# Two edits to the order of a two-layer graph network: where the differences of the gate weights are queued, and how many gate graphs the third group runs among the next layers

## The chip, the cores and the metric

The kernel runs on one core of a Trainium2 chip. The metric is device microseconds of one execution; the figure given for a kernel is the median of its runs. The engines are called as the profile calls them: PE (matrix products, with PEld for its weight loads), DVE (vector), ACT (scalar), POOL and SP, whose queue issues most of the transfers.

## The reference, cut to what matters

64 graphs of 256 nodes with 256 features pass two layers, each with a residual and a layer norm.

```
# layer 0
h = (norm_adj + max(alpha, 1e-10) * I) @ x;  x = layernorm(x + h @ W.T + b)
# layer 1
h  = relu(bn1(conv1(x)))                       # 1x1
xc = relu(bn2(conv2(h)) + x)                   # 17 taps along the nodes
s  = x @ w_se.T + b_se;  A = exp(-|s_i - s_j|^2) * adj
xm = A @ relu(x @ w_msg.T + b_msg)
gi = concat(xc, xm) @ w_ih.T + b_ih;  gh = x @ w_hh.T + b_hh
r = sigmoid(gi_r + gh_r);  z = sigmoid(gi_z + gh_z);  n = tanh(gi_n + r * gh_n)
x  = layernorm(x + (1 - z) * n + z * x)
```

All is float32.

## The kernel before, in words

The 64 graphs are worked in `NQ = 4` groups of `Q = 16`. For a group there are three kinds of work.

- **Layers**: `layer0(g)` and `layer1(g)` for each graph. `layer1` ends with the message part `xn` written to DRAM, and leaves the forward transform of `h` in `V`. Its products are in order `p_x1T`, `p_conv`, `p_msg`, `p_dft`, `p_rows`, `p_dist`, `p_nmp`; those of `layer0` are `p_adjT`, `p_hT`, `p_out` (L398, read by DVE at L403).
- **Transform**: the 17-tap convolution is a product in frequency space, `products(step)` for 12 steps (`p_real`, `p_k`, with the transformed taps `u` streamed from DRAM), and then an inverse transform on DVE, `real_transform`, `complex_begin` and `complex_end`. The last has 58 pieces, called `end`, and writes `xc_d`.
- **Gates**: `gru(g)` for each graph, in four pieces (`yield` ends one): `p_rz` products, more of them with the transposes `p_xcT` of the next graph, and two halves `p_n`. The first graph of a group has four pieces more, which load its inputs. For `p_rz` a product of two by two blocks is done with seven block products in place of eight; that needs sums of the inputs (`sums`, on POOL) and differences of the weights (`T1` to `T4` of `wrz`, four DVE instructions at L948), made once.

The pieces of different kinds are interleaved by hand, with generators. In `graphs(first, part, V, others)`, which runs the layers of the graphs in `part`, a piece of `others[i]` is called after the first and the sixth piece of `layer1`, and pieces of `layer0` of the graph two further on after the second, fifth and sixth. `take(stage, n)` gives n pieces of a stage. In the first group, `others` holds the 13 parts of the transformed taps (`weights`), for graphs 0 to 12, and one piece of `gate_weights` for each of the graphs 13, 14 and 15: the loads of the weights, an empty piece, and the differences.

The text order gives each instruction its rank. A planner then fixes the order on each engine before the run: where an engine has nothing of higher rank ready by the planner's own costs, an instruction of lower rank that is ready goes first. [...] `with tc.issue_after(i):` ties each instruction of its block behind `i` on `i`'s engine. `mark(op)` puts certain DVE instructions on the list `marks`: in `layer0` the two at L403, in `layer1` those of `h`, `msg` and `aT`, and in `gru` five, among them `first` (L809). `paced(main, end, rate)` empties the list after each piece of `main` and ties `rate` pieces of `end` behind each mark on it; outside `paced` the list only grows.

After the transform of group q come the layers of group q+1 from graph `AHEAD` on, with the first gates of group q (`early`) in `others`: five pieces a call for q = 0, two for q = 1 and 2. What `early` leaves follows at once. The other gates of group q (`late`) run in the transform of group q+1: some pieces between the steps of its products (for the last group one at each odd step, six in all), the rest as `main` of `paced`. For the last group `main` is `late` alone, at 1.35 pieces for each mark:

```
elif more:
    run(paced(chain(merge(take(late, 20), take(begin, 6), 3), begin), end, RATES[q]))
else:
    run(paced(late, end, RATES[q]))
    run(end)
```

`AHEAD` is 12 for the second group and 6 for the third and fourth; the gates of the last group run at the end, alone.

Of the kernel before, what the change touches and what calls it, by code (L numbers as in the profile page):

```python
# [20 lines left out]
def bcast_rows(v, n, rows=P):  # L21

    return bass.AP(tensor=v.tensor, offset=v.offset, ap=[[0, rows], [1, n]])
# [3 lines left out]
def kernel(  # L27
# [27 lines left out]
    nc = tc.nc  # L55
# [10 lines left out]
    Q = P // GT  # L66
# [20 lines left out]
    marks = []  # L87
# [7 lines left out]
    def load(g):  # L95
        if g >= B:
            return
        ain[g] = loads.tile([P, NCH, N], F32, name="adj_t")
        nc.sync.dma_start(ain[g], adj[g].rearrange("(c p) m -> p c m", p=P))
        xin[g] = loads.tile([P, NCH, D], F32, name="x_t")  # L100
        nc.sync.dma_start(xin[g], x[g].rearrange("(c p) f -> p c f", p=P))
# [40 lines left out]
    wrz = const.tile([P, 7, HALF, D], F32)  # L142
    B11, B21, B22, T1, T2, T3, T4 = range(7)
# [116 lines left out]
    def load_taps(pool, n):  # L260

        if n == NPARTS:
            return
        ng = GW // NPARTS
        tp = TAPS_OF[n] = pool.tile([KT, ng, D], F32, name="taps", bufs=2)

        def taps(c, t, count, step):

            channel = min(c * GW + n * ng, D - ng)
            return bass.AP(  # L270
                tensor=conv2T.tensor, offset=conv2T.offset + (channel * TAPS + t) * D,
                ap=[[step * D, count], [TAPS * D, ng], [1, D]],
            )

        for c in range(GC):
            nc.sync.dma_start(tp[c * TR : (c + 1) * TR], taps(c, 0, TR, 1))
        nc.sync.dma_start(tp[GC * TR : KT - 1], taps(0, TR, GC - 1, GW * TAPS))
        nc.sync.dma_start(tp[KT - 1 :], taps(GC - 1, TR, 1, 1))
# [461 lines left out]
    def load_conv(g):  # L740
        CONV[g] = gate.tile([P, NCH, D], F32, name="xc_g")
        nc.sync.dma_start(CONV[g], xc_d[g // Q][g % Q].rearrange("(c p) d -> p c d", p=P))
# [8 lines left out]
    def residual(g):  # L751

        nc.gpsimd.dma_start(  # L753
            CONV[g], x1_d[g // Q][g % Q].rearrange("(c p) d -> p c d", p=P), accum_op=ALU.add
        )
# [108 lines left out]
    def merge(main, other, every=1):  # L864

        for i, _ in enumerate(main):
            yield
            if i % every == every - 1 and next(other, "end") != "end":
                yield
        yield from other  # L870
# [5 lines left out]
    def take(stage, n):  # L876

        for _ in range(n):
            if next(stage, "end") == "end":
                return  # L880
            yield
# [6 lines left out]
    def run(stage):  # L888
        for _ in stage:
            pass  # L890
# [18 lines left out]
    def graphs(first, part, V, others):  # L909


        for i in part:
            load(first + i + 3)
            given = {"layer0": layer0(first + i + 2) if first + i + 2 < B else iter(()), "other": others[i]}
            for piece, _ in enumerate(layer1(first + i, V, i)):
                yield
                for name in PLACES[piece]:
                    if next(given[name], "end") != "end":
                        yield
            yield from given["other"]  # L920

    with tc.tile_pool(name="setup", bufs=1) as setup:
        load_taps(setup, 0)
        nc.sync.dma_start(wmsg, w_msgT.rearrange("(k p) o -> p k o", p=P))
        nc.sync.dma_start(bmsg_t, bcast_rows(b_msg, D))
        firsts = merge(layer0(0), layer0(1))
        run(take(firsts, 2))
        load(2)
        tables(setup)
        run(firsts)  # L930
        scale2 = next(batch_norms(setup))

        def gate_weights():
            for b, half_inputs, cols in ((B11, 0, 0), (T1, 0, 1), (B21, 1, 0), (B22, 1, 1)):
                at = slice(cols * D, (cols + 1) * D)
                if half_inputs == 0:
                    parts = ((slice(0, DCH), w_hhT), (slice(DCH, HALF), w_ihT[D : D + P]))
                else:
                    parts = ((slice(0, 1), w_ihT[D + P :]), (slice(1, HALF), w_ihT[:D]))
                for k, w in parts:  # L940
                    nc.sync.dma_start(wrz[:, b, k], w[:, at].rearrange("(k p) o -> p k o", p=P))
            for k, w in ((0, w_hhT), (DCH, w_ihT[D:]), (2 * DCH, w_ihT[:D])):
                nc.sync.dma_start(wn[:, k : k + DCH], w[:, 2 * D :].rearrange("(k p) o -> p k o", p=P))
            yield
            yield

            for to, a, b in ((T3, B22, T1), (T1, T1, B11), (T2, B22, T1), (T4, B21, T2)):
                nc.vector.tensor_sub(wrz[:, to], wrz[:, a], wrz[:, b])  # L948
            yield

        more_weights = gate_weights()
        others = [weights(setup, i, scale2) for i in range(NPARTS)]
        others += [take(more_weights, 1) for i in range(NPARTS, Q)]
        run(graphs(0, range(Q), V, others))
        bih_t = setup.tile([P, 3 * D], F32, name="bih", tag="taps", bufs=2)
        nc.sync.dma_start(bih_t, bcast_rows(b_ih, 3 * D))
        bhh_t = setup.tile([P, 3 * D], F32, name="bhh", tag="taps", bufs=2)
        nc.sync.dma_start(bhh_t, bcast_rows(b_hh, 3 * D))
        brz = brz_t.rearrange("p i d -> p (i d)")
        nc.vector.tensor_add(brz, bih_t[:, : 2 * D], bhh_t[:, : 2 * D])  # L960
        nc.vector.tensor_sub(brz_t[:, 1], brz_t[:, 1], brz_t[:, 0])
        nc.vector.tensor_copy(bn_t[:, 0, :], bih_t[:, 2 * D :])
        nc.vector.tensor_copy(bn_t[:, 1, :], bhh_t[:, 2 * D :])
    ustream = ctx.enter_context(tc.tile_pool(name="ustream", bufs=6))
    EARLY = 4

    def open_ahead(graphs):

# [4 lines left out]
    def gates(q, part):  # L973

        for i in part:
            if i == 0:
                load_conv(q * Q)
                load_gate(q * Q)
                yield
                load_conv(q * Q + 1)  # L980
                residual(q * Q)
                yield
                transposed(q * Q)
                yield
                input_sums(q * Q)
                yield
            yield from gru(q * Q + i)

    def nothing():
        return iter(())  # L990
# [5 lines left out]
    late = nothing()  # L996
    for q in range(NQ):
        first = (q + 1) * Q
        more = q + 1 < NQ
        end = complex_end(q)  # L1000
        if more:
            if q:
                others = [take(late, 3 if i % 3 == 0 else 2) for i in range(AHEAD)]
            else:
                others = [nothing() for _ in range(AHEAD)]
            begin = graphs(first, range(AHEAD), V2, others)
        sums(0)
        real = real_transform()
        for step in range(STEPS):
            if step < 4:  # L1010
                run(products(step))
            else:
                run(merge(products(step), take(real, 1)))
                run(complex_begin(step))
            if q:
                run(take(late, (0, 1, 1, 1, 1, 1, 2, 1, 2, 1, 2, 1)[step] if more else step % 2))
            else:
                run(take(begin, 3))
        run(real)
        if not q:  # L1020
            run(paced(begin, end, RATES[q]))
# [5 lines that stand above are left out]
        if more:  # L1027
            run(late)
            run(end)
            for f in range(0, FL, 12):  # L1030
                nc.scalar.copy(V[:, f : f + 12, :, : AHEAD * GT], V2[:, f : f + 12])
            if q == 0:
                scope.close()
                gate = ctx.enter_context(tc.tile_pool(name="gate", bufs=2))
            early = gates(q, range(EARLY))
            others = [take(early, 5 if q == 0 else 2) for _ in range(Q)]
            run(graphs(first, range(AHEAD, Q), V, others))
            run(early)
            if q == 0:
                scope, AHEAD, V2 = open_ahead(6)  # L1040
                ctx.enter_context(scope)
            late = gates(q, range(EARLY, Q))
        else:
            run(gates(q, range(Q)))

# [52 lines left out]
```

## Time and profile before

| | |
|---|---|
| median of 3 runs | 2172.98 us (2172.46 to 2173.61) |
| profiled execution | 2174.33 us |
| its span, first to last instruction | 2172.5 us |
| mean granted PE clock | 0.989 |
| PE, DVE, ACT, POOL busy | 2064.0, 1550.7, 834.3, 664.2 us |
| HBM traffic | 200.62 MB read, 103.06 MB written |

A row of groups gives line, engine, operation, output and inputs, then count, busy time and mean duration. A row of waits names who waited for whom, with total, number and longest. A row of the timeline has start, duration, engine and line, and in brackets the idle time before it and what ended it. Rows of windows give a stretch's length and each engine's busy time in it. Matmul ends are modelled, so distances between starts say more than durations.

### The profile page before, as it was taken

What the parts mean: (1) busy time and instruction counts of PE and PEld (TensorE: products, weight loads), DVE (VectorE), ACT (ScalarE), POOL (GpSimd) and SP (SyncE); (2) the same over time, 40 slices, a digit from 0 to 9 for tenths busy, and PEclk for the clock granted to TensorE, in tenths of its full rate; (3) what the DMA queues carried; (4) which work ended last, traced back from release to release, by engine and by line L of the source; (5) the groups of instructions that cost most, each with busy time, mean ns of one, the idle gap of its engine ahead of it and who ended that gap; (6) DMA issues with size and microseconds to landing.
All of it is one profiled execution on the core that took longest, in us unless ns stands there. A gap on an engine that the chain in (4) does not pass through costs nothing. (4 is left out here: it accounts for less than half of the span.)

```text
span 2172.5 us, 29034 instructions
## 1 busy us (share of the span) xinstructions
PE 2064.0 (95%) x9805; PEld 1748.4 (80%) x9805; DVE 1550.7 (71%) x3691; ACT 834.3 (38%) x1847; POOL 664.2 (31%) x640
## 2 busy tenths in 40 slices
PE   7999999887999999999999999899999998999998
PEld 5788788776788887788888888778888887788887
DVE  5555568785568798775556989775555889977776
ACT  4566643455331122455453122346543112222222
POOL 2444310211431233313222133323231123444442
PEclk9999999999999999999999999999999999999999
DMA  4765656434337644344335754334334844444442
GB/s 129 223 194 178 216 185 207 154 125 141 97 112 226 194 123 122 107 119 121 104 99 175 208 163 116 110 117 132 101 97 124 250 117 122 120 123 107 112 101 60
DMA packets 251182, 305.65 MB, mean 141 GB/s; under 512 B 18174, under 2 KB 229714, under 8 KB 251034
## 3 DMA queue, kind: packets, MB, share of 16 engines
q1 hardware_dynamic: 183530, 200.46, 30.4%
q10 hardware_dynamic: 44480, 67.39, 8.7%
q0 software_dynamic: 23024, 35.95, 8.6%
q8 instruction: 78, 1.28, 0.2%
q14 instruction: 70, 0.57, 0.1%
HBM read 200.62 MB, written 103.06 MB: 140 GB/s over the span
## 5 line engine op out<-in xcount | busy, mean ns | idle before, releaser
L833 PE MATMUL p_n<-wn,inputs 128*128 128x256 f32 x1536 | 355.9, 385 | 11.0 <-DVE first L809 10.6
L796 PE MATMUL p_rz<-wrz,sums 128*128 128x256 f32 x1536 | 350.9, 382 | 3.2 <-POOL sums L775 2.3
L833 PEld LDWEIGHTS p_n<-wn,inputs 128*128 128x128 f32 x1536 | 289.1, 192 | 58.1 <-DVE first L809 14.5
L796 PEld LDWEIGHTS p_rz<-wrz,sums 128*128 128x128 f32 x1536 | 290.7, 191 | 48.2 <-issue 5.9
L796 PE MATMUL p_rz<-wrz,inputs 128*128 128x256 f32 x1152 | 271.7, 379 | 0.4 <-ACT inputs L766 0.4
L314 POOL TENSOR_TENSOR ln_rs<-ln_rs,neg_half 128x2 f32<-128x2 f32 x129 | 101.2, 784 | 527.9 <-DVE ln_rs L313 417.4
L796 PEld LDWEIGHTS p_rz<-wrz,inputs 128*128 128x128 f32 x1152 | 217.5, 190 | 30.3 <-ACT inputs L766 1.0
L845 ACT ACTIVATE nn<-gn 128x256 f32<-128x256 f32 x128 | 53.2, 416 | 333.2 <-DVE gn L842 333.0
L518 PE MATMUL p_k<-u,VM 128*128 128x256 f32 x736 | 175.3, 380 | 4.1 <-DMA u<-ud 3.3
L775 POOL TENSOR_TENSOR sums<-inputs 128x384 f32<-128x384 f32 x64 | 67.8, 1059 | 335.1 <-ACT inputs L766 327.0
L358 POOL TENSOR_TENSOR dis<-deg,neg_half 128x2 f32<-128x2 f32 x64 | 46.5, 726 | 402.6 <-DVE deg L356 395.6
L324 ACT ACTIVATE x_g<-x_g,ln_mr,ln_rs 128x256 f32<-128x256 f32 x128 | 70.0, 593 | 245.6 <-DVE ln_mr L322 242.0
L518 PEld LDWEIGHTS p_k<-u,VM 128*128 128x128 f32 x736 | 138.1, 190 | 25.7 <-DMA u<-ud 3.4
L428 PE MATMUL p_conv<-wc,xn 128*128 128x259 f32 x512 | 128.8, 394 | 19.6 <-ACT xn L420 18.5
L388 PE MATMUL p_hT<-adjT,x 128*128 128x256 f32 x512 | 126.6, 390 | 9.5 <-DVE msg L452 4.9
L381 POOL TENSOR_TENSOR x_t<-x_t,b_t 128x512 f32<-128x512 f32 x64 | 86.4, 1350 | 146.7 <-ACT x L380 89.3
L463 PE MATMUL p_dft<-fwd,h 128*128 128x240 f32 x512 | 117.8, 373 | 13.9 <-ACT h L432 13.0
L428 PEld LDWEIGHTS p_conv<-wc,xn 128*128 128x128 f32 x512 | 97.1, 194 | 39.8 <-ACT xn L420 24.1
L489 DVE TENSOR_TENSOR aT<-aT,adjT 128x512 f32<-128x512 f32 x64 | 44.3, 692 | 115.3 <-ACT aT L488 115.3
L398 PE MATMUL p_out<-w,hT 128*128 128x256 f32 x512 | 123.9, 385 | 2.5 <-ACT hT L393 2.1
L449 PE MATMUL p_msg<-wmsg,xn 128*128 128x256 f32 x512 | 121.3, 379 | 0.0
L494 PE MATMUL p_nmp<-aT,msg 128*128 128x256 f32 x512 | 121.1, 379 | 0.2 <-DVE aT L489 0.2
(154 smaller groups left out, 3894.9 us busy)
## 6 DMA issues: line engine op xcount, KB each, us to landing
u<-ud SPq DMA_DIRECT2D x284, 256.0 KB
xn_d<-xn ACTq DMA_DIRECT2D x64, 512.0 KB
inputs<-xn_d SPq DMA_DIRECT2D x64, 512.0 KB
ud<-u_set POOLq DMA_DIRECT2D x39, 480.0 KB, 6.2
adj_t<-in_adj_dram SPq DMA_DIRECT2D x64, 256.0 KB
x_t<-in_x_dram SPq DMA_DIRECT2D x64, 256.0 KB
x_d<-x ACTq DMA_DIRECT2D x64, 256.0 KB
xc_d<-VM SPq DMA_DIRECT2D x64, 256.0 KB
```

The source lines that it names most:

```text
L314: nc.gpsimd.tensor_tensor(rs[:, : len(chunks)], rs[:, : len(chunks)], neg_half[:, : len(chunks)], op=ALU.pow)
L324: nc.scalar.activation(y[:, c, :], y[:, c, :], AF.Identity, bias=mr[:, c : c + 1], scale=rs[:, c : c + 1])
L381: nc.gpsimd.tensor_tensor(x_t, x_t, b0_t.unsqueeze(1).to_broadcast([P, NCH, D]), op=ALU.add)
L388: nc.tensor.matmul(p[:, k, :], x1[:, mc, k * P : (k + 1) * P], adjT[:, mc, 1 - mc : 3 - mc, :].rearrange("p n q -> p (n q)"), start=mc == ...
L398: nc.tensor.matmul(p[:, c, :], hT[:, k, c * P : (c + 1) * P], w0[:, k, :], start=k == 0, stop=k == DCH - 1)
L428: nc.tensor.matmul(p, x1T[:, k, c * P : (c + 1) * P], wc1[:, k, :], start=k == 0, stop=k == DCH - 1)
L449: nc.tensor.matmul(p[:, c, :], x1T[:, k, c * P : (c + 1) * P], wmsg[:, k, :], start=k == 0, stop=k == DCH - 1)
L463: nc.tensor.matmul(p[:, t0 * FL : t1 * FL], h[:, c, k * P : (k + 1) * P], fwd[:, first : first + t1 - t0, :].rearrange("p t f -> p (t f)") ...
L494: nc.tensor.matmul(p[:, k, :], msg[:, mc, k * P : (k + 1) * P], aT[:, mc].rearrange("p n q -> p (n q)"), start=mc == 0, stop=mc == NCH - 1,)
L518: nc.tensor.matmul(p[:, j * D : (j + 1) * D], v[:, k, :], u[:, k, :], start=k == 0, stop=k == DCH - 1)
L796: nc.tensor.matmul(p[:, j * D : (j + 1) * D], a[:, k], wrz[:, b, k], start=k == 0, stop=k == HALF - 1)
L833: nc.tensor.matmul(p[:, o * D : (o + 1) * D], lhsT, w, start=j == 0, stop=j == len(part) - 1)
```

## The change

The four differences of the gate weights are put into a block that ties them behind the last mark on the list at that point of the text. `EARLY`, the number of graphs whose gates run among the next layers, becomes a tuple by group: 4, 4 and, for the third group, 3. That group's fourth graph, number 35, becomes the first of `late`.

```diff
@@ -944,8 +944,9 @@
-            for to, a, b in ((T3, B22, T1), (T1, T1, B11), (T2, B22, T1), (T4, B21, T2)):
-                nc.vector.tensor_sub(wrz[:, to], wrz[:, a], wrz[:, b])
+            with tc.issue_after(marks[-1]):
+                for to, a, b in ((T3, B22, T1), (T1, T1, B11), (T2, B22, T1), (T4, B21, T2)):
+                    nc.vector.tensor_sub(wrz[:, to], wrz[:, a], wrz[:, b])
             yield
@@ -962,7 +963,7 @@
-    EARLY = 4
+    EARLY = (4, 4, 3)
@@ -1032,14 +1033,14 @@
-            early = gates(q, range(EARLY))
+            early = gates(q, range(EARLY[q]))
             others = [take(early, 5 if q == 0 else 2) for _ in range(Q)]
             run(graphs(first, range(AHEAD, Q), V, others))
             run(early)
...
-            late = gates(q, range(EARLY, Q))
+            late = gates(q, range(EARLY[q], Q))
```

## The prediction

> **What bounds the kernel now.** I read the page's busy times first, then the windows of single stages, then the waits inside the two stages that the change touches, and last the timeline of those places.
>
> ```profile
> PE 2064.0 (95%) x9805; PEld 1748.4 (80%) x9805; DVE 1550.7 (71%) x3691; ACT 834.3 (38%) x1847; POOL 664.2 (31%) x640
> ```
>
> TensorE is busy 95% of the span, so only its idle time (2172.5 - 2064.0 = 108.5 us) and its slow-clock time can be won, and whatever the change does must show as a gap on PE. The windows below (length; busy us of PE, PEld, DVE, ACT, POOL; PE clock; DMA share; GB/s) show where gaps are.
>
> ```profile
> 98.12:119.61 21.49, 17.88 (x80) 14.26 (x79) 13.97 (x32) 10.16 (x23) 8.12 (x8) 0.92 0.60 168
> 119.61:135.26 15.65, 15.65 (x79) 13.21 (x78) 8.84 (x25) 9.86 (x23) 7.70 (x9) 1.00 0.67 201
> 135.26:151.30 16.04, 15.93 (x79) 13.14 (x78) 8.79 (x24) 9.86 (x23) 7.36 (x8) 1.00 0.63 196
> ...
> 274.57:288.33 13.76, 12.78 (x63) 10.38 (x62) 7.89 (x25) 8.04 (x19) 2.65 (x3) 1.00 0.31 97
> ...
> 1590.00:1638.55 48.55, 47.79 (x233) 39.98 (x232) 27.03 (x71) 22.55 (x53) 11.62 (x12) 1.00 0.27 82
> ...
> 1802.00:1912.27 110.27, 100.12 (x460) 86.03 (x461) 103.86 (x223) 25.54 (x54) 41.26 (x37) 0.98 0.44 119
> ...
> 1930.70:2160.00 229.30, 229.30 (x1091) 201.57 (x1092) 164.03 (x313) 59.35 (x124) 100.80 (x93) 1.00 0.39 100
> ```
>
> The first three run from one graph's first transpose (`p_x1T`) to the next's. A graph with a weight part costs 16.04 us in steady state; one graph at 98 us takes 21.49, at a mean clock of 0.92. The others are: graph 15 of the first group, whose DVE is idle 13.76 - 7.89 = 5.87 us; the third group's gates among the last layers (PE 98%, DVE 56%); the late gates beside the last inverse transform (DVE 94%, PE short by 10.15 us); and the last gates alone (PE full).
>
> Why the graph at 98 us is long: the waits of DVE and of PE between 80 and 125 us, each with total, times, longest:
>
> ```profile
> DVE wrz L948 <- DMA wrz<-in_w_ihT_dram: 4.9, 1, 4.9
> ```
> ```profile
> PE p_dft L463 <- ACT h L432: 2.5, 1, 2.5
> PE p_conv L428 <- DVE x L403: 1.1, 1, 1.1
> ```
>
> And in the timeline (start, duration):
>
> ```profile
> 99.42 0.96 DVE L948 TENSOR_TENSOR wrz<-wrz 128x768 f32<-128x768 f32 x1 [4.91 <-DMA wrz<-in_w_ihT_dram]
> 100.29 1.22 DVE L298 TENSOR_TENSOR u_set<-u_set,u_set 120x1024 f32<-120x1024 f32 x1
> 101.54 0.88 DVE L403 SCALAR_TENSOR_TENSOR x<-p_out,dis,x_t 128x256 f32<-128x256 f32 x2
> ```
>
> The planner took the four differences, written in graph 15 (about 275 us), and put them 175 us early, as filler. The first stands at the head of DVE's queue until the weights land. Behind it lie L298, L403 and the layer norm after it, with their data there (`p_out` was issued from 94.67). PE then waits for a bank that L403 frees, and for `h`, 3.6 us together, and comes back slow: eight `p_hT` matmuls take 2.99 us at 110.78 where a steady graph has 1.89.
>
> [...] L298's last input was copied by 95.91 and it ran at 100.29. [...] I therefore price PE by start-to-start distances, and not by its 95%.
>
> **Part 1, the differences.** Nothing is added or removed; four DVE subtracts (0.95 us each, 3.8 together) and two semaphore instructions of DVE's sequencer are tied behind `marks[-1]`. When the block is traced, graph 14 has just emitted the third piece of `layer0(16)`, so that mark is the second L403 of that piece, at 273.1 to 274.0 us. The eleven weight loads on SP are outside the block and stay at 72 to 111 us; nothing moves on SP, ACT or POOL.
> Gain: the stretch from 82.46 (one graph's transpose) to 151.30 holds four graphs: 68.84 us against 4 x 16.04 = 64.16, so 4.68 us. This contains the gaps, the slow clock and the differences' own DVE time. With them gone, nothing else is late there: the next waits on DVE (1.0 to 2.1 us for ACT and POOL) stand in every steady graph.
> Cost: in graph 15 the weights landed 170 us ago, so there is no new wait; the first reader is `p_rz` at 543.6. DVE's gaps after the mark are 1.13 us (waiting for POOL's power), 0.67, 0.45, 1.05 and 1.90; a 0.95 us subtract fits in the larger ones. Behind each subtract could stand `h` (L431), `dist_r` or `aT`, for which ACT and PE wait. Bounds: 0 if all fit; 3.8 if each delays PE by its full length; below nothing is excluded, since no work goes. I take 0: cover is the 5.87 us of idle DVE. Without it, up to 3.8.
>
> **Part 2, one gate graph.** `EARLY` is 4, 4, 3: graph 35 (third group's fourth) leaves `early` for `late`. Each gate graph is four pieces and the first has four more: 4 x 4 + 4 = 20 pieces, two at each of 10 graphs, were exactly used up; now 16 pieces end at graph 61, and layers of 62 and 63 have none written beside them (nor a `layer0`, since 64 does not exist). No instruction is added: 14.69 us of PE (distance of `p_xcT` in the last stage), 229.3 us of that stage hold 15.6 graphs so 164.03/15.6 = 10.5 us of DVE, three 256 or 512 KB loads on SP, one accumulating load and five or so adds and powers on POOL, one store on ACT move from a stage with DMA at 0.27 to one at 0.44. SP's loads move past the last transform's `u` loads; PE waits for those were 1.3 us in 1470 to 1757, so ±1.3.
> In program order PE's time is moved, not saved: -14.69 in the layers, +14.69 in the late gates. What can differ is PE's idle time.
> Layers alone: from graph 14's starts a layers period is 13.59 us; without layer0's fillers the wait from `p_rows` to `p_dist` can shrink from 2.33 to 1.61 us and `p_dist` to `p_nmp` from 2.57 to 2.35, so 12.65, with 13.59 - 0.9 idle - 4.17 of layer0 = 8.5 us of PE work. Uncovered that is 4.1 us a graph, 8.3 for two. But the planner fills such gaps by readiness. In graph 62 today:
>
> ```profile
> 1649.27 0.38 PE L476 MATMUL p_rows<-ident,scols 128*128 128x128 f32 x2
> 1649.49 1.46 PE L796 MATMUL p_rz<-wrz,sums 128*128 128x256 f32 x6
> 1650.88 0.70 PE L487 MATMUL p_dist<-dist_r,dist_l 32*128 32x256 f32 x4
> 1651.51 1.56 PE L796 MATMUL p_rz<-wrz,sums 128*128 128x256 f32 x6
> ```
>
> Six gate matmuls, written after `p_dist`, stand before it. Graph 35's inputs are ready when graph 34 ends (about 1636), so as `late` work it can be drawn into the same gaps. I take 0 for the tail, bounds 0 to +8.3.
> In the late stage PE waits for DVE:
>
> ```profile
> PE p_n L833 <- DVE first L809: 10.3, 8, 2.4
> ```
>
> The pacing hangs 1.35 pieces of the transform on each of a gate graph's five marks: 58 / 1.35 / 5 = 8.6 graphs, before as after. The 13th graph comes after these, where PE is full. So 0, bounds -3.4 (a third of the 10.15 us filled, my guess at what more ready work could do) to +10.5.
>
> **Sum.** The profiled execution took 2174.33 us, span 2172.5 and 1.83 around it: 2174.33 - 4.68 + 0 + 0 = 2169.65. It lies 1.35 above the median of the runs, so the forecast is 2172.98 - 4.68 = **2168.3**.
>
> **The cases.** A measurement can tell about 0.2% (4.35 us) from no change: the borders are 2168.6 and 2177.3.
> - A, 0.45: stall gone, both costs hidden: 2168.3, give or take 1.5; 0.27 of it beyond the border, 0.18 within.
> - B, 0.25: the stall goes, and part returns: the tail runs half bare (+4.1) or the subtracts delay `h`: 2169 to 2174, no change to tell. For it: graphs 13 to 15, without weight parts, show 0.73 us PE gaps before `p_conv`. Against it: the filling above.
> - C, 0.20: as A, and the late stage's gaps shrink by 3.4: about 2164.9, faster. For it: the last transform can start earlier. Against: the pacing is unchanged.
> - D, 0.10, slower: the moved graph's 10.5 us of DVE leave a stage with DVE at 56% and join the stretch from 1711 to 1912 where DVE sets the pace; if all shows, 2168.3 + 10.5 = 2178.8. It decides only when 9.0 us of the 10.5 show (4.68 + 4.35). Against it: graphs enter in order and 8.6 of them meet the transform either way.
> - That the change does not do what it says (the mark being earlier than I think) would leave the stall: near 2173, inside B.
>
> Faster 0.47, same 0.43, slower 0.10. The range, 2163.5 to 2174.5, takes in A, B and C's centre with its size uncertain; D and the far ends are left out.
>
> **What would show it.** L948 after 273 us, no DMA wait on it; the graph at 98 us about 16 us long, clock near 1.00; graph 15 at most 0.5 us over 13.76. In the tail, `p_rz` or `p_n` matmuls between the pieces of graphs 62 and 63, PE idle under 2 us there; the wait of `p_n` for `first` still near 10 us. Wrong, if those two graphs show gaps of 1 to 2 us with nothing between, if graph 15 grows by microseconds, or if that wait moves by more than 3.

## The result, and the profile after

The kernel became slower. The median of 14 runs is 2178.45 us (2175.13 to 2183.98), against 2173.39 us of the 14 runs of the kernel before beside it: a ratio of 1.003, with a 95% interval of 1.0023 to 1.0038 (the quotient of these two medians is 1.0023, that of the means 1.0028). That is beyond the 0.2% that a measurement can tell from no change, and outside the range of the prediction. The profiled execution took 2183.98 us (span 2182.2), 5.5 us above the median, so its own distances are read below, not its total.

The page's first part, busy time of each engine, hardly moves; PE gains 7.2 us of busy time at the same count of matmuls:

```profile
PE 2071.2 (95%) x9805; PEld 1753.8 (80%) x9805; DVE 1551.2 (71%) x3691; ACT 834.1 (38%) x1847; POOL 665.2 (30%) x640
```

More busy time for the same 9805 matmuls can only be matmuls that took longer. The windows of the kernel after (length; busy us of PE, PEld, DVE, ACT, POOL; PE clock; DMA share; GB/s) show where. They are cut like those of before, from `p_x1T` to `p_x1T`, and the last one is the last gates alone. The two at 1638 and 1653 are graphs 62 and 63, the end of the layers that lost its gate graph.

```profile
98.24:114.27 16.03, 15.92 (x79) 13.13 (x78) 8.79 (x23) 9.86 (x23) 7.47 (x7) 1.00 0.75 231
114.27:129.93 15.66, 15.66 (x79) 13.21 (x78) 8.95 (x25) 9.85 (x23) 7.71 (x9) 1.00 0.65 201
...
1638.58:1653.68 15.10, 10.72 (x43) 8.08 (x42) 5.82 (x23) 6.42 (x13) 1.40 (x2) 0.86 0.25 87
1653.68:1668.66 14.98, 14.15 (x55) 10.85 (x54) 5.03 (x13) 4.75 (x10) 0.00 (x0) 0.80 0.25 80
...
1939.80:2169.10 229.30, 229.30 (x1094) 201.79 (x1093) 164.08 (x313) 59.31 (x124) 100.80 (x93) 1.00 0.39 101
```

The same two graphs in the kernel before, whose gates still lay between their pieces:

```profile
1638.55:1656.37 17.82, 17.82 (x89) 15.23 (x88) 9.19 (x28) 7.86 (x17) 1.44 (x3) 1.00 0.24 78
1656.37:1670.33 13.96, 13.80 (x67) 11.37 (x66) 8.38 (x18) 4.97 (x12) 5.36 (x5) 1.00 0.32 82
```

The graph at 98 us now takes 16.03 us instead of 21.49: part 1 did there what the prediction says. The differences run in graph 15, without a wait (first and last of the four; start, duration):

```profile
269.33 0.93 DVE L949 TENSOR_TENSOR wrz<-wrz 128x768 f32<-128x768 f32 x1
...
273.33 0.95 DVE L949 TENSOR_TENSOR wrz<-wrz 128x768 f32<-128x768 f32 x1
```

Graphs 62 and 63 issue 98 matmuls where 156 stood before, and yet take 30.08 us against 31.78, at clocks of 0.86 and 0.80. PE's waits of the kernel after from 1636 to 1670 us (total, times, longest):

```profile
PE p_nmp L494 <- DVE aT L489: 1.8, 2, 1.6
PE p_conv L428 <- ACT xn L420: 1.4, 2, 0.7
PE p_dist L487 <- DVE dist_r L480: 1.1, 1, 1.1
PE p_dft L463 <- ACT h L432: 0.9, 1, 0.9
```

Together 5.2 us. And its timeline of PE (start, duration, and in brackets the idle time before):

```profile
1638.58 0.60 PE L419 MATMUL p_x1T<-ident,x 128*128 128x128 f32 x4
1639.90 2.02 PE L428 MATMUL p_conv<-wc,xn 128*128 128x259 f32 x8 [0.73 <-ACT xn L420]
1641.76 1.89 PE L449 MATMUL p_msg<-wmsg,xn 128*128 128x256 f32 x8
1644.58 1.89 PE L463 MATMUL p_dft<-fwd,h 128*128 128x240 f32 x8 [0.93 <-ACT h L432]
1646.31 0.38 PE L476 MATMUL p_rows<-ident,scols 128*128 128x128 f32 x2
1647.76 0.70 PE L487 MATMUL p_dist<-dist_r,dist_l 32*128 32x256 f32 x4 [1.07 <-DVE dist_r L480]
1650.11 3.78 PE L494 MATMUL p_nmp<-aT,msg 128*128 128x256 f32 x8 [1.65 <-DVE aT L489]
...
1655.42 3.82 PE L428 MATMUL p_conv<-wc,xn 128*128 128x259 f32 x8 [0.67 <-ACT xn L420]
...
1662.99 1.56 PE L518 MATMUL p_real<-u,VM 128*128 128x256 f32 x6
```

There is no `p_rz` or `p_n` anywhere between the pieces. After the four gaps of graph 62 the eight matmuls of `p_nmp` take 3.78 us where they took 1.89 in the kernel before, and the `p_conv` of graph 63 take 3.82 where those of graph 62 took 2.02. The clock's record in the trace is at one half from 1649.3 for 10.2 us (0.50 in the window 1649.3 to 1659.5). PE is busy in 8.8 of these, so 4.4 us of work are lost (the rest lies in gaps already counted). Idle 5.2 and half clock 4.4 make 9.6 us. Set against the same program with all four graphs early (`e1_differences_only`, below), the gate work stands 2.4 us later at 1616 us and 12.4 us later in the last stage: about 10 us were lost in between, in these two executions. The tail that part 2 left bare is where the time went.

### The profile page after: what moved, and what is told of

It reads as the page before. It is cut to its first block, busy times and chain, and to the rows that moved or that the text cites. A ratio compares the mean times of both kernels' runs of the same rounds, so it can differ in the third digit from the quotient of the medians.

```text
span 2182.2 us, 29037 instructions
## 1 busy us (share of the span) xinstructions
PE 2071.2 (95%) x9805; PEld 1753.8 (80%) x9805; DVE 1551.2 (71%) x3691; ACT 834.1 (38%) x1847; POOL 665.2 (30%) x640
```

## The experiments

Two theories on the result. **Theory A:** part 2 alone makes the loss, in the bare tail of graphs 62 and 63, and nothing fills that tail because something other than readiness keeps the moved graph out. **Theory B**, the prediction's rival D: the moved graph's DVE work loads the DVE-bound stretch of the last transform. A third question is where the 4.68 us of part 1 are. A and B have other meanings in the prediction's cases and in experiment 10. The expectations below are as written before each run; ratios are to the kernel before, run beside it, with 95% intervals.

**1. Part 1 alone.**

```diff
-    EARLY = (4, 4, 3)
+    EARLY = (4, 4, 4)
```

> The differences tied behind the mark, EARLY left at 4, 4, 4. Theory (the loss is the third group's bare tail, and the differences gain what the stall cost): about 4 us faster than before, ratio 0.998 (0.9975 to 0.9985). Rival (the gain of the differences is given back before the gates start, as the profile after shows between 490 and 546 us): ratio 1.000. Rival (the differences in their new place delay the layers of graph 15): ratio 1.000 to 1.002, and graph 15 over 14.5 us long.

Measured: 0.9993 (0.9985 to 1.0001), 2170.48 us. About 1.5 us are gained, hardly to be told from nothing, though the graph at 98 us takes 16.03 us here too. Graph 15 takes 14.29 us, where it took 13.76.

**2. Part 2 alone.** The kernel before, with three early graphs for the third group.

```diff
-    EARLY = 4
+    EARLY = (4, 4, 3)
...
-            early = gates(q, range(EARLY))
+            early = gates(q, range(EARLY[q]))
...
-            late = gates(q, range(EARLY, Q))
+            late = gates(q, range(EARLY[q], Q))
```

> EARLY 4, 4, 3, the differences left where they were. Theory (bare tail of graphs 62 and 63): 7 to 10 us slower than before, ratio 1.003 to 1.0045; PE gaps and half-clock time in the layers of those two graphs, and the stall at 98 us still there. Rival (the moved graph's 10.5 us of DVE slow the last transform): the same total, but with PE's waits for DVE between 1711 and 1912 longer by that, and the two graphs' layers not.

Measured: 1.0032 (1.0019 to 1.0045), 2180.06 us. The whole loss is here. PE's waits in the tail are those of the kernel after to the tenth (1.8, 1.4, 1.1, 0.9), and a half clock of 10.2 us begins at 1647.1. In the last transform the wait of `p_n` for `first`, which theory B would lengthen, is 9.2 us, against 10.3 before. The product of the two parts, 0.9993 x 1.0032 = 1.0025, lies in the interval of the whole.

**3. Three early graphs, begun later.** The graph stays among the late gates; the 16 pieces that are left start at call 8 of the layers and so reach the end.

```diff
-            others = [take(early, 5 if q == 0 else 2) for _ in range(Q)]
+            others = [take(early, 5 if q == 0 else 2) if q < 2 or i >= 8 else nothing() for i in range(Q)]
```

> The change, but the third group's gate pieces start two graphs later (none beside graphs 54 and 55, two a graph from 56 to 63). Graph 35 is in the late gates as in the change. Theory (bare tail): the loss goes, since 62 and 63 have gate matmuls again and 54 and 55 have layer0; ratio to before 0.998 to 1.000. Rival (DVE of the moved graph): still as slow as the change, ratio 1.002 to 1.004.

Measured: 0.9998 (0.999 to 1.0006), 2171.25 us. In the tail one wait of 0.2 us for `aT` is left. Graph 35 is as late as in the changed kernel, so its lateness costs nothing that shows; the bare tail is what differs. This speaks against theory B, as does the wait that B would have lengthened. PE's waits of the kernel after from 1757 to 2000 us:

```profile
PE p_n L833 <- DVE first L809: 10.2, 8, 2.4
```

It was 10.3 before, and is 11.6 in this run: nowhere near 10.5 us longer.

**4. What keeps the moved graph out.** The planner takes ready work of lower rank for an idle engine, and graph 35 was ready. But its matmuls need a buffer of PSUM from the pool behind `accbank`, which has four, and so do the products of the last transform, which the text has ahead of it. This run gives the last group's products buffers of the other pool, and changes nothing else.

```diff
-    def products(step):
+    def products(step, accbank=accbank):
...
-                run(products(step))
+                run(products(step, accbank if more else bank))
...
-                run(merge(products(step), take(real, 1)))
+                run(merge(products(step, accbank if more else bank), take(real, 1)))
```

> The change, but the last group's products take their PSUM banks from the layers' pool, not from the gates'. Theory (the late gates could not be drawn into the tail's gaps because the products, written before them, have the first claim on the gates' banks): gate matmuls p_rz stand between the pieces of graphs 62 and 63, PE idle there under 2 us, and most of the loss goes: ratio to before 0.998 to 1.000. Rival (the planner does not reach that far whatever the banks): bare tail and ratio near 1.0025 as in the change. Rival (DVE of the moved graph): gates drawn into the tail, yet ratio near 1.0025.

Measured: 0.9998 (0.999 to 1.0006), 2170.59 us. Its timeline of PE:

```profile
1641.78 0.38 PE L476 MATMUL p_rows<-ident,scols 128*128 128x128 f32 x2
1642.00 0.60 PE L796 MATMUL p_rz<-wrz,inputs 128*128 128x256 f32 x2
1642.44 1.03 PE L796 MATMUL p_rz<-wrz,sums 128*128 128x256 f32 x4
1643.39 0.70 PE L487 MATMUL p_dist<-dist_r,dist_l 32*128 32x256 f32 x4
1644.02 2.43 PE L796 MATMUL p_rz<-wrz,sums 128*128 128x256 f32 x10
1646.29 1.89 PE L494 MATMUL p_nmp<-aT,msg 128*128 128x256 f32 x8
```

Now the moved graph does what the prediction expected: its `p_rz` stand before and after `p_dist`, no half clock falls there, and the loss is gone. So readiness was not what was missing. With one pool for both, the products, first in the text, have the claim on its buffers, and their inputs come only with graph 63; in the kernel after, the first of them (`p_real`) fill one gap of graph 63 from 1662.99 and none of graph 62. That the claim is by text order is the reading that fits this run and the next; the planner's choice itself was not recorded, so this step is argued, while the shared buffers as the obstacle are shown.

**5. The fourth graph early, but written after the layers.** Part 1 with four early graphs, of which the last four pieces stand in `run(early)`, behind the layers and ahead of the products.

```diff
-    EARLY = (4, 4, 3)
+    EARLY = (4, 4, 4)
...
-            others = [take(early, 5 if q == 0 else 2) for _ in range(Q)]
+            others = [take(early, 5 if q == 0 else 2) if q < 2 or i < 14 else nothing() for i in range(Q)]
```

> The differences tied as in the change; four graphs' gates in the third group's early ones, but none written beside the layers of 62 and 63: graph 35's pieces follow these layers in the text, ahead of the last group's products. Theory (the planner fills the tail with gates if they rank before the products that claim the same banks): p_rz and p_n between the pieces of 62 and 63, no half-clock time near 1648 us, ratio to before 0.998 to 1.000. Rival (only pieces written between the layers can fill them): bare tail, ratio near 1.0025.

Measured: 1.0004 (0.9996 to 1.0013), 2172.12 us. No half clock in the tail; what PE waits there is 0.6 us for `h`, 0.6 for a load of `u` and 0.2. Graph 62 in its timeline of PE:

```profile
1644.28 0.60 PE L796 MATMUL p_rz<-wrz,inputs 128*128 128x256 f32 x2
1644.71 1.03 PE L796 MATMUL p_rz<-wrz,sums 128*128 128x256 f32 x4
1645.67 0.70 PE L487 MATMUL p_dist<-dist_r,dist_l 32*128 32x256 f32 x4
1646.30 2.43 PE L796 MATMUL p_rz<-wrz,sums 128*128 128x256 f32 x10
```

Ahead of the products in the text, the gates are drawn into the layers, although they are written after them. With the buffers shared, a place in the text ahead of the products was enough; a place among the layers was not needed.

**6. A second graph moved.**

```diff
-    EARLY = (4, 4, 3)
+    EARLY = (4, 4, 2)
```

> The change with 4, 4, 2: a second gate graph moved, so that graphs 60 to 63 have no gate pieces beside them; 60 and 61 still have layer0 of 62 and 63. Theory (the loss is the bare tail of the two graphs without layer0): the second graph adds only the 0.9 us of idle time a graph that layers with layer0 alone show, 1 to 3 us more than the change, ratio to before 1.003 to 1.005. Rival (each moved graph costs its DVE time in the last transform): about as much again, ratio 1.006 to 1.008.

Measured: 1.0048 (1.0035 to 1.006), 2181.07 us: by the ratios 0.0018 or about 4 us more than the kernel after, and by the medians 2.6, not 8 to 10 again; the two intervals touch, so the size is rough. Graphs 60 and 61, now bare of gates as well, take 14.19 and 13.65 us, against the 13.59 of a layers period with `layer0`: their `layer0` of graphs 62 and 63 still covers most of it. A moved graph is dear where nothing else lies beside the layers.

**7. The differences at another place.** Part 1 costs something in graph 15, so here they are tied to an instruction beside graph 8 instead.

```diff
-            with tc.issue_after(marks[-1]):
+            with tc.issue_after(DIAGONAL[10]):
...
-    EARLY = (4, 4, 3)
+    EARLY = (4, 4, 4)
```

> EARLY 4, 4, 4; the differences tied behind layer0(10)'s diagonal, about 150 us, where the weight parts fill PE. Theory (the new place at graph 15 costs 0.5 us, the rest of the missing gain is half-clock time between 490 and 546 us): no DMA wait before the differences, no loss at graph 15, total within 1 us of the differences alone: ratio to before 0.9985 to 0.9995. Rival (the new place eats the gain): ratio 0.998 or less.

Measured: 0.9994 (0.9986 to 1.0002), 2170.31 us. They run at 168.9 to 174.8 us without a wait, and graph 15 takes 13.65 us, against 14.29 in `e1_differences_only`. The 0.6 us do not show in the time (0.9994 against 0.9993), so the new place is at most a small part of what ate the gain.

**8. Where the rest of part 1's gain goes.** From the `p_x1T` at 490 us to the third one after it, the profiled kernel before takes 55.98 us; the seven profiled executions with the differences moved and ACT's copies kept take 57.8 to 59.6. In that stretch PE waits for `xn`, which stands behind two copies of `V` on ACT's queue (4.12 us together in `e8_differences_at_graph_8`). This run moves the copies to DVE, on top of run 7.

```diff
-                nc.scalar.copy(V[:, f : f + 12, :, : AHEAD * GT], V2[:, f : f + 12])
+                nc.vector.tensor_copy(V[:, f : f + 12, :, : AHEAD * GT], V2[:, f : f + 12])
```

> As the run with the differences at graph 8, and the copies of the ahead graphs' transforms into V on DVE, not ACT. In the runs so far PE waits 7.6 us at 521 us for an ACT copy behind three of them (2.1 us each), and the clock halves there. Theory (the gain of the differences is small because what follows until the first gates is bound by ACT and DVE and runs at half clock in part, so time must be taken out there): that wait falls to under 3 us, ratio to before 0.996 to 0.9985. Rival (the first gates wait for the transform's last store, so PE's wait only moves): ratio as without this edit, 0.9985 to 0.9995.

Measured: 0.997 (0.996 to 0.9979), 2165.23 us (2162.55 to 2167.35), the lowest median of all and ahead of both kernels. PE's waits for `xn` from 500 to 545 us, first with the copies on ACT (`e8_differences_at_graph_8`):

```profile
PE p_conv L428 <- ACT xn L420: 7.4, 2, 6.7
```

and then with them on DVE:

```profile
PE p_conv L428 <- ACT xn L420: 1.5, 2, 0.7
```

The longest wait fell by 6.0 us. This is a gain of its own, and does not say what the rest of part 1's gain met.

**9. The copies alone.** The same edit on the kernel before.

> The kernel before with only the copies into V on DVE. If the wait at 521 us is worth what it seemed beside the moved differences (about 5 us), ratio to before 0.997 to 0.9985; with the moved differences it was 0.997. If the two add up fully, 0.9985 and the differences are worth 3 us there; if the copies alone give all of it, 0.997.

Measured: 0.9977 (0.9969 to 0.9984), 2167.29 us. Divided out of run 8, the differences are worth 0.997 / 0.9977 = 0.9993 here too: 1.5 us, the third time (0.9993, 0.9994, 0.9993), though none of the three is clear of zero by itself.

**10. Other executions of the kernel before.** Three more profiled executions, unchanged, to see whether the half clock near 495 us belongs to the moved differences, and how long the stall at 98 us is otherwise.

> The kernel before, unchanged, for a second trace. Open: the gain of the differences is there at 490 us in every trace with them moved, and partly gone at 546; all eight such traces show half-clock time starting between 494 and 497 us, the two without do not. Theory A (the earlier arrival causes it): no half-clock time between 485 and 515 us here. Theory B (it comes and goes in every kernel): half-clock time there in about half of the looks at the kernel before.

> The kernel before, unchanged, a third trace. As for the look before: theory A no half-clock time between 485 and 515 us, theory B in about half of the looks.

> The kernel before, unchanged, a fourth trace. As for the looks before: theory A no half-clock time between 485 and 515 us, theory B in about half of the looks.

Measured: 2175.87, 2173.98 and 2173.22 us. The wait of L948 for the weights is 2.9, 3.3 and 3.2 us here, not 4.9. The graph at 98 us takes 20.07, 18.58 and 18.59 us, not 21.49. With part 2 alone and with the copies alone, which leave the stall in, it takes 19.28 and 18.59. Over the steady 16.03 the six traces give 5.5, 4.0, 2.6, 2.6, 3.3 and 2.6 us, on average 3.4; a half clock of 3.4 us in that graph is in the first two.

The stretch at 490 us tells a second thing. The same instructions between the same marks of two of these traces, windows as above; the first:

```profile
487.90:506.80 18.90, 16.20 (x63) 12.10 (x62) 13.31 (x40) 8.14 (x19) 2.81 (x3) 0.82 0.23 70
```

and the second:

```profile
487.10:502.90 15.80, 13.05 (x63) 10.16 (x62) 12.98 (x38) 8.13 (x19) 2.81 (x3) 1.00 0.28 84
```

Sixty-three matmuls either way, with the same gaps of 0.7, 0.5 and 1.5 us among them, and 3.1 us apart by the clock. Of the four traces of the kernel before, two have a half clock there, and two have none; part 2 alone and the copies alone, with the differences at their old place, have none. So it is two of six, against all eight traces with the differences moved. Theory A of this half clock fails as written, since it comes without the move as well, and theory B does not explain eight of eight.

The same gaps, then, came with a half clock in one execution and without one in the other: after them the eight `p_out` matmuls take 3.78 us in the first and 1.99 in the second. No run tested what decides between the two, nor why the half clock came in all eight traces with the differences moved, by their earlier arrival or by chance.

## Why the prediction was wrong

**Part 1, the mechanism: right.** L949 runs at 269.3 to 274.3 us without a wait, the graph at 98 us takes 16.03 us at a clock of 1.00, and nothing else was late there.

**Part 1, the gain: mis-sized.** The term 4.68 us came from one execution, whose stall was the longest of the six seen, with a half clock of 3.4 us besides; three of the six lie at 2.6 us and the mean is 3.4. (Its yardstick of 4 x 16.04 us was high too: with the stall gone the four graphs take 63.4 to 63.7, not 64.16.) The total moved by 1.5 us, three times alike. Of the difference, the cost in graph 15, taken as 0, is 0.5 us there (14.29 against 13.76, about the "at most 0.5" of the prediction), but running the differences elsewhere did not win it. The half clock near 495 us (3.4 to 6.8 us long, so 1.7 to 3.4 us of work lost) is in eight of eight traces with the differences moved and in two of six without. The stretch of 490 us takes 58.8 us on average in the seven traces with the differences moved and ACT's copies kept, and 57.3 in the five with the differences at their old place and these copies kept: 1.5 us more. With it a rough account closes, from a few executions each: 3.4 - 0.5 - 1.5 = 1.4 us, against 1.5 measured. That the moved differences cause the 1.5 us is not shown; it stays open.

**Part 2, the tail: the step that failed.** "As `late` work it can be drawn into the same gaps. I take 0 for the tail." The six gate matmuls that the prediction shows before `p_dist` were written ahead of the transform's products; the moved graph is written behind them and shares their buffers. Readiness was looked at, the claim on buffers was not. Run 4 shows it by taking the products out of that pool: the loss of 0.0032 goes. The prediction's own sign of being wrong, gaps of 1 to 2 us in those two graphs with nothing between, is what the profile shows, at 1.07 and 1.65 us.

**The bound on the tail: too low.** The 8.3 us were idle time at full clock, 4.1 a graph. Graph 62 has 4.4 us of it, but graph 63 only 0.8, as `p_real` covered a part of it; so the idle time came out lower, at 5.2 us. The layers' own work met the estimate: 30.08 - 9.6 us, less 3.3 for twelve matmuls of the products, is 8.6 a graph, against 8.5. But with the gaps came a half clock of 10.2 us, which lost 4.4 us of work and which the prediction had priced for the stall at 98 us and left out here. Over the runs, the mean of (1 - clock) x 2170 us is 24.0 us in `e1_differences_only` and 29.4 in the kernel after, and 8.0 us lie between their medians.

**Part 2, the late stage: right.** Cost 0 was taken and nothing shows: the wait of `p_n` for `first` is 10.2 against 10.3 (9.2 to 11.6 in the other runs with one graph moved), and runs 3 and 4 keep graph 35 late without loss.

**The rivals.** Rival B named this tail, half bare with +4.1; the tail was wholly bare in graph 62, and B's price lacked the clock. Rival D gave the sign, but by a mechanism that two runs and the unchanged wait speak against. The forecast had the right effects on its list; their sum, -1.5 + 7, came out on the other side since the gain was a third of its price and the cost was taken at nothing.

## What to carry to other kernels

Before filler work is moved out of a stage, look which part of that stage has no other cover, and ask of the work meant to slide in not only whether its inputs are ready but which finite buffers it must claim, and who stands ahead of it in that claim. Where the traces show a half clock after gaps, price a gap with the slow time that follows it, not with its idle time alone: here 4.4 us of gaps in graph 62 came with 10.2 us at half clock, which lost another 4.4 us of work. And take the size of a stall that waits for a DMA from several executions: one trace here gave 4.68 us, and three of six give 2.6.

## What the runs showed of the hardware

In the bare tail a half clock came with gaps of which none was longer than 1.65 us. In graph 62 of the kernel after, PE waits 0.73, 0.93, 1.07 and 1.65 us, the clock is at one half from 1649.3 us for 10.2 us, and the eight `p_nmp` matmuls take 3.78 us, against 1.89 at a clock of 1.00 in the kernel before. The gaps of 1.07 and 1.65 us stand in `e6_two_early` too, after one of 0.73 us; the half clock there lasts 3.4 us, and the eight `p_nmp` take 3.38 us. No run tested what sets its length. In the runs of the kernel before, with PE busy 95%, (1 - clock) x 2170 us is 24 us on average; this bounds what the half clock costs from above, since PE waits in part of it.

A copy of 128x2304 in f32 takes 2.1 us on ACT (`e8_differences_at_graph_8`) and 1.35 us on DVE (`e7_copies_of_v_on_dve`), and with these copies moved from ACT's queue to DVE's 0.0023 of the whole time went (`e10_copies_on_dve_only`).
